# All four heads of a group in every stretch of scores, one PSUM bank for each row quarter

## The chip, the cores and the metric

The kernel runs on one core of one Trainium2 chip. The time is the device time of one execution in microseconds (us); lower is better. An execution is one launch that computes the whole output.

## The reference

The input is x with shape (16, 512, 512): 16 batches of 512 tokens with 512 channels, fp32. The block is attention and a gated feed-forward layer, each between two layer norms:

```python
x = x + layernorm(attention(layernorm(x)))
x = x + layernorm(ffn(layernorm(x)))

# attention, 32 heads of 16 channels
q, k, v = (h @ Wq.T + bq), (h @ Wk.T + bk), (h @ Wv.T + bv)
q, k = rope(rope(q, absolute), temporal), rope(rope(k, absolute), temporal)
scores = q @ k.T / 4                       # causal: -inf above the diagonal
out = softmax(scores) @ v                  # then out @ Wo.T + bo

# ffn, 1408 inner channels; gate, up and down weights are -1, 0 or 1
out = (silu((x @ gate.T) * gate_s) * ((x @ up.T) * up_s)) @ down.T * down_s
```

## The kernel before

**Heads and scores.** A head has 16 channels. Four heads make a group, and there are 8 groups a batch, 128 in all. In SBUF a head stands in 32 of the 128 partitions (a row quarter): q is held as a high and a low part (`q2`), k as two tiles, `kh` and `kl`. So a score matmul has 32 rows, and four of them, one for each row quarter, run in the array side by side. For each head two kinds of scores are computed. `S` (tile `s`, query rows on the partitions) serves only to find each query's maximum: one matmul with `kh`, one with `kl`. `ST` (tile `st`, key rows on the partitions) is what goes into the exponential: `kh`, `kl`, and a third matmul of ones with `mx`, the negated maxima as rows, so that exp needs no other operand. Only blocks on or below the causal diagonal are computed: 512+384+256+128 = 1280 columns for each head and kind.

**Stretches.** A group takes six steps (`STEPS`, `one_step`, L792). In a step, `scores` (L562) handles ST of two heads of group n (`pair`) and S of the other two row quarters' heads of a later group m, n+1 or n+2. A third of the columns is done in a pair of steps (`S_SETS`, `ST_SETS`). `st` has two PSUM banks and one buffer, `s` two buffers of one bank, `av` one bank, and three banks (`ps_d`, tag "d") are shared by all dense products and transposes. After the matmuls, `weights` (L631) takes exp of `st` on ScalarE into `pt` and zeroes the part above the diagonal on GpSimd; `maxima` (L607) adds the mask to `s`, negates and takes the minimum in one custom VectorE operation a block, which is two instructions in the profile (the operation and the read of its accumulator). When all of a group's maxima are there, `turn_maxima` (L617) transposes them on TensorE (`pm`), splits them into two parts (`nmh`, `nml`) and a step later sends them into `mx` by DMA. `values` (L649) multiplies the weights with `v17`, which has a column of ones for the sums, into `av`.

**Dense work.** Between the scores of two steps, and before `values`, stands a share of the other work. `dense`, `gate_ups` and `downs` write it as a list of pieces with costs (an fp32 matmul of 512 columns is 1.0, an fp32r one 0.27, a transpose 0.15), and `run_list` (L696) hands out equal shares of the sum over a batch's 48 steps. The list of batch b holds, in this order: v and q products of batch b+1, o (the attention's output product) of b-1, k of b+1 with the transposes for the feed-forward layer of b-1, gate/up of b-1, down of b-1 with the norm of b+2. A `merge` puts follow-up work on the other engines a given cost later. The tail of a q or k product (`qk_block`, L329) is two bias operations into `ys` on ScalarE, the product with the cosines into `ya` on VectorE and with the sines on GpSimd; its rest adds the two and splits the sum (`yh`, `yl`). The tail of a gate product is tanh on ScalarE and a product on VectorE, that of an up product one VectorE operation into `ht`.

**Order.** Every instruction is kept in program order on its engine (`InOrder`, L39; its line 49 is the line that the profile shows for nearly all instructions). Queue, buffers and order are therefore fixed by the sequence in which the Python code emits them. All loads and stores but three are issued by SyncE (SP).

**Weights.** `load_w` (L227) loads a projection in two halves of 512 KB into four buffers "w"; `load_wf` (L398) loads gate and up weights of 128 inner channels, 512 KB, into three buffers "wf".

**Two arms.** `front` prepares batches 0 and 1 and checks that the three ternary matrices are exact in fp32r; the kernel then runs one of two arms of the program. The profiled one is the `exact` arm, in which gate/up and down are pairs of fp32r matmuls with high and low parts (`xntf`, `xntfl`; `hh`, `hl`).

Of the kernel before, what the change touches and what calls it, by code (L numbers as in the profile page):

```python
# [28 lines left out]
STEPS = 6  # L29
# [5 lines left out]
S_SETS = [[(3, 0, 512)], [(0, 384, 128), (2, 0, 384)], [(1, 0, 256)]]  # L35
ST_SETS = [[(0, 0, 512)], [(3, 0, 128), (1, 128, 384)], [(2, 0, 256)]]
# [17 lines left out]
class Block:  # L54
# [15 lines left out]
    def __init__(self, tc, ctx, a):  # L70
# [15 lines left out]
        self.ps_s = pool("ps_s", bufs=2, space=bass.MemoryType.PSUM)  # L86
        self.ps_t = pool("ps_t", bufs=1, space=bass.MemoryType.PSUM)
# [22 lines left out]
    def constants(self):  # L110
# [13 lines left out]
        for half in range(2):  # L124
            self.load_w(0, "q", half)
        for tb in range(NB):
            self.load_x(1, tb, "x1", 4)
        for half in range(2):
            self.load_w(0, "k", half)
# [5 lines left out]
        for name in ("bo", "dscale"):  # L135
# [6 lines left out]
        self.mask = con.tile([P, T], mybir.dt.bfloat16, tag="mask", name="mask")  # L142
        nc.gpsimd.memset(self.mask, 0.0)
        m = self.mask[:, T - P : T]
        nc.gpsimd.affine_select(
            out=m, in_=m, compare_op=ALU.is_ge, fill=-BIG, base=0, pattern=[[-1, P]], channel_multiplier=1
        )
# [19 lines left out]
        self.odd = con.tile([P, 2 * self.NF], FP, tag="odd", name="odd")  # L167
# [5 lines left out]
    def load_checks(self):  # L173

        a, n = self.a, 2 * NC * P
        ht = self.tile([P, self.NF, T], "ht", bufs=1).rearrange("p f t -> p (f t)")
        xl = self.tile([P, NC, T], "xntfl", bufs=1).rearrange("p c t -> p (c t)")
        places = [ht[:, ts(i, n)] for i in range(self.NF * T // n)] + [xl[:, ts(i, n)] for i in range(NC * T // n)]
        small = [tag for tag, k in (("oc", 4), ("q2", 3), ("kh", 3), ("kl", 3)) for _ in range(k)]
        self.wgu0, self.wd0 = [], []  # L180

        def load(f):
            w = places.pop() if 3 <= f < self.NF - 1 else self.tile([P, n], "wf", bufs=3)
            self.sp.dma_start(out=w, in_=a["wgu"][f].rearrange("p w c j -> p (w c j)"))
            self.wgu0.append(w)

        for f in range(self.NF - 1):
            load(f)
        for f in range(self.NF):
            tag = small.pop()  # L190
            w = self.tile([P, C], tag, bufs=4 if tag == "oc" else 3)
            self.sp.dma_start(out=w, in_=a["wd"][ts(f, P), :])
            self.wd0.append(w)
        self.load_last = lambda: load(self.NF - 1)

    def check_weights(self):

        def check(i, w, r):  # L200
            self.act.copy(r, w)
            self.dve.scalar_tensor_tensor(w, w, 1.0, r, ALU.mult, ALU.not_equal, accum_out=self.odd[:, i : i + 1])

        def gate_up(f):
            if f == 1:
                self.load_last()
            w = self.wgu0[f]
            check(f, w, self.tile(list(w.shape), "pt", bufs=4, dtype=FR))

        def down(f):  # L210
            check(self.NF + f, self.wd0[f], self.wd[:, f, :])
# [15 lines left out]
    def load_w(self, b, name, half):  # L227

        t = self.tile([P, NC, C // 2] if name in "qk" else [P, NC // 2, C], "w", bufs=4)
        self.sp.dma_start(out=t, in_=self.a["w" + name][half])  # L230
        self.wts[b, name, half] = t
# [73 lines left out]
    def v_block(self, b, tb):  # L305
# [6 lines left out]
        return self.product("pv", NC, lambda c: self.xnts["a", b][:, c, ts(tb, P)], lambda c: self.wts[b, "v", c // 2][:, c % 2, :], tail)  # L312

    def fold_bias(self):
# [3 lines left out]
        def tail(p):  # L318
# [6 lines left out]
            lambda c: self.wts[-1, "o", c // 2][:, c % 2, :],  # L325
# [3 lines left out]
    def qk_block(self, b, name, c):  # L329
# [20 lines left out]
        def store():  # L350
# [10 lines left out]
            "p" + name, NC, lambda i: self.wts[b, name, c // 2][:, i, ts(c % 2, P)], lambda i: self.xnts["a", b][:, i, :], tail  # L361
        ), rest, store

    def o_block(self, b, tb):
# [19 lines left out]
        def rest_3():  # L384
# [5 lines left out]
            "po", NC, lambda c: self.ocs[b, c][:, ts(tb, P)], lambda c: self.wts[b, "o", c // 2][:, c % 2, :], tail  # L390
# [7 lines left out]
    def load_wf(self, b, f):  # L398
        if self.exact:
            t = self.tile([P, 2, NC, P], "wf", bufs=3, dtype=FR)  # L400
            self.sp.dma_start(out=t.bitcast(FP), in_=self.wgs[f])
        else:
            t = self.tile([P, 2, NC, P], "wf", bufs=3)
            self.sp.dma_start(out=t, in_=self.a["wgu"][f])
        self.wfs[b, f] = t

    def gate_up(self, b, f):
# [14 lines left out]
        if self.exact:  # L422
            x = lambda i: self.xnts["f", b][i % 2][:, i // 2, :]
            w = lambda k: (lambda i: self.wfs[b, f][:, k, i // 2, :])
# [3 lines left out]
        g = self.product("pg", NC, lambda c: self.wfs[b, f][:, 0, c, :], x, tail_g)  # L428
        u = self.product("pu", NC, lambda c: self.wfs[b, f][:, 1, c, :], x, tail_u)
# [67 lines left out]
    def dense(self, b, between=()):  # L497
# [13 lines left out]
        if nxt:  # L511
            for tb in range(NB):
                L += self.v_block(bn, tb)
            for c in range(NC):
                if c < 2:
                    do(self.load_w, o, "o", c)
                qk("q", c)
                if c % 2:
                    do(self.load_w, bn, "k", c // 2)
        else:  # L520
            for half in range(2):
                do(self.load_w, o, "o", half)
        later = []
        if old:
            do(self.load_xr, o, 0)
            do(self.load_xr, o, 1)
            for tb in range(NB):
                items, *rests = self.o_block(o, tb)
                L += items
                for r, k in zip(rests, (3.5, 6.5, 9.5)):  # L530
                    if r is rests[2] and tb >= 2 and nxt:
                        later.append(r)
                    else:
                        self.merge(L, r, k, ("f", tb))
        L += between
# [26 lines left out]
    def scores(self, n, m, i):  # L562

        third, pair = divmod(i, 2)
        ps = pm = None
        todo = []
        if 0 <= n < self.B * NG:
            ps = self.ps_t.tile([P, 2, T], FP, tag="st", name="st")
            q, ks, mx = self.qs[n], self.ks[n], self.mxs[n]
            for j in range(2):  # L570
                h = 32 * (2 * pair + j)
                r, r2 = slice(h, h + 32), slice(h, h + 2)
                todo.append([])
                for kb, at, w in ST_SETS[third]:
                    out, x = ps[:, j, at : at + w], q[r, T - w : T]
# [3 lines left out]
                        (out, self.one[r2, :], mx[r2, T - w : T], False, True),  # L579
                    ]  # L580
        if 0 <= m < self.B * NG:
            if n < 0 and i % 2:
                both = self.ps_t.tile([P, 2, T], FP, tag="st", name="st")
                pm = [both[:, j, :] for j in range(2)]
            else:
                pm = [self.ps_s.tile([P, T], FP, tag="s", name="s") for _ in range(2)]
            q, ks = self.qs[m], self.ks[m]
            for j in range(2):
                h = 32 * (2 * (1 - pair) + j)
                r = slice(h, h + 32)  # L590
                todo.append([])
                for qb, at, w in S_SETS[third]:
                    out, x = pm[j][:, at : at + w], q[r, ts(qb, P)]
                    todo[-1] += [(out, x, ks[0][r, 0:w], True, False), (out, x, ks[1][r, 0:w], False, True)]

        for k in range(max((len(t) for t in todo), default=0)):
            for t in todo:
                if k < len(t):
                    out, l, r, first, last = t[k]
                    self.pe.matmul(out, l, r, start=first, stop=last)  # L600
        if ps is not None:
            self.weights(n, third, pair, ps)
        if pm is not None:
            for j in range(2):
                self.maxima(m, third, 2 * (1 - pair) + j, pm[j])

    def maxima(self, m, third, j, s):  # L607
        if m not in self.nms:
            self.nms[m] = self.tile([P, 4, NB], "nm", bufs=2)
        for qb, at, w in S_SETS[third]:  # L610
            x = s[:, at : at + w]
            self.dve.tensor_tensor_reduce(
                out=x, in0=x, in1=self.mask[:, T - w : T], scale=-1.0, scalar=BIG, op0=ALU.add, op1=ALU.min,
                accum_out=self.nms[m][:, j, qb : qb + 1],
            )

    def turn_maxima(self, m):  # L617
        p = self.psum("pm")
        self.pe.transpose(p[0:16, 0:P], self.nms.pop(m).rearrange("p j b -> p (j b)"), self.ident)
# [11 lines left out]
    def weights(self, n, third, pair, ps):  # L631
        w = sum(w for _, _, w in ST_SETS[third])
        if third < 2 or pair == 0:
            pt = self.tile([P, 2, T], "pt", bufs=4)
            self.pts[n, third, pair] = pt
        if third == 2:
            if pair:
                pt = self.pts[n, 2, 1] = self.pts[n, 2, 0]
            pt = pt[:, pair, :].rearrange("p (j t) -> p j t", j=2)
        self.act.activation(pt[:, :, :w], ps[:, :, :w], AF.Exp, scale=0.25)  # L640
        if third == 1:
            d = pt[:, :, 0 : 2 * P]
            pat = [[0, 2], [0, 2], [1, P]]
        else:
            d = pt[:, :, 0:P]
            pat = [[0, 2], [1, P]]
        self.pool.affine_select(out=d, in_=d, compare_op=ALU.is_ge, fill=0.0, base=0, pattern=pat, channel_multiplier=-1)

    def values(self, n, third):  # L649
        b, g = divmod(n, NG)  # L650
        if third == 0:
            self.avs[n] = self.ps_av.tile([P, T], FP, tag="av", name="av")
        av = self.avs[n]
        for kb, at, w in ST_SETS[third]:
            for j in range(4):
                h = 4 * g + j
                pt = self.pts[n, third, j // 2]
# [381 lines left out]
```

## Time and profile before

| | before |
|---|---|
| median of 3 runs | 3214.8 us (3213.17 to 3222.2) |
| the profiled execution's own time | 3215.86 us |
| its span in the profile | 3214.0 us |
| granted TensorE clock | 0.984 |
| TensorE busy | 96% |
| VectorE, ScalarE, GpSimd busy | 59%, 48%, 43% |
| DMA, share of 16 engines | 43.1% |
| score matmuls with `s` and `st` | 10212 |
| exp `pt<-st`, 128x1024 and 128x512 | 512 of 1024 ns, 256 of 596 ns |
| maxima `s<-s,mask`, and accumulator reads | 2034 of 510 ns, 2048 of 141 ns |

PE is TensorE's matmuls, PEld its weight loads (they run beside matmuls), DVE VectorE, ACT ScalarE, POOL GpSimd, SP the queue that issues DMAs. A group's name is output<-inputs by the program's tile names. A row's busy time is the union of its instructions' times; the mean of one includes its pipeline latency, so for matmuls that follow each other the distance of their starts says more than their length. Times in a timeline are microseconds from the span's start.

### The profile page before, as it was taken

To read this page: it belongs to the slowest core of one execution; us is meant where nothing else is said; L and a number is where in the kernel's file an instruction comes from. 1 tells how busy PE (TensorE), PEld (TensorE's weight loads), DVE (VectorE), ACT (ScalarE), POOL (GpSimd) and SP (SyncE) were. 2 spreads that over 40 slices of the span, in tenths; PEclk is the share of its full clock that TensorE was granted. 3 is DMA by queue.
4 is the path that set the end of the run, shared out by engine and by line. 5 is a ranking of instruction groups with operands and counts; after the bars stand their busy time and mean duration, and the time that the engine had idled before them with its cause. 6 is when DMAs were issued, how large, how long until landed. Compare 5 with 4: busy or idle time off the path is not lost.

```text
span 3214.0 us, 59287 instructions
## 1 busy us (share of the span) xinstructions
PE 3097.9 (96%) x21258; PEld 1743.3 (54%) x21258; DVE 1888.0 (59%) x5911; ACT 1542.7 (48%) x2243; POOL 1383.9 (43%) x1933
## 2 busy tenths in 40 slices
PE   6889999999999999999999999999999999999988
PEld 2334555646556464655646455464655646455556
DVE  5465656556565665656566565665656566565633
ACT  5354545454554544545454554544455454453432
POOL 4143445443544534345443544534345453443343
PEclk9899999999999999999999999999999999999999
DMA  6454534445353443525345352543535345343422
GB/s 251 166 166 152 189 101 163 139 149 172 108 190 106 160 164 123 195 93 177 127 152 173 127 185 96 168 147 123 195 101 183 122 147 172 123 156 105 131 97 71
DMA packets 227441, 471.41 MB, mean 147 GB/s; under 512 B 40976, under 2 KB 45072, under 8 KB 226704
## 3 DMA queue, kind: packets, MB, share of 16 engines
q1 hardware_dynamic: 226704, 466.47, 43.1%
q8 instruction: 170, 2.79, 0.4%
q10 hardware_dynamic: 432, 1.05, 0.1%
q14 instruction: 135, 1.11, 0.1%
HBM read 345.79 MB, written 125.30 MB: 147 GB/s over the span
## 4 chain that ended last, share of the span: by engine, by line
PE 83%; DVE 2%; DMA 2%; ACT 2%; POOL 1%; issue 1%; SPq 0%; ACTq 0%; DVEq 0%; POOLq 0%
PE st L49 16%; PE pu L49 11%; PE pg L49 10%; PE av L49 9%; PE pd L49 9%; PE po L49 7%; PE pq L49 6%; PE pv L49 5%; PE pk L49 5%; PE s L49 3%; DMA kl<-kd 2%; PE px L49 1%; ACT pt L49 1%; DVE s L49 1%; PE pm L49 1%
## 5 line engine op out<-in xcount | busy, mean ns | idle before, releaser
L49 DVE CUSTOM_DVE_ANT_0 s<-s,mask 128x512 f32<-128x512 f32 (+1 forms) x2034 | 974.9, 510 | 713.8 <-PE s L49 530.8
L49 ACT ACTIVATE pt<-st 128x1024 f32<-128x1024 f32 (+1 forms) x768 | 677.0, 882 | 755.9 <-PE st L49 746.9
L49 POOL TENSOR_SCALAR_AFFINE_SELECT pt<-pt 128x256 f32<-128x256 f32 (+1 forms) x768 | 393.8, 513 | 1202.3 <-ACT pt L49 1200.0
L49 PEld LDWEIGHTS st<-q,kh 32*128 32x128 f32 x2048 | 191.3, 183 | 463.3 <-issue 225.6
L49 PE MATMUL st<-q,kh 32*128 32x512 f32 (+3 forms) x2048 | 411.2, 398 | 22.3 <-ACT pt L49 20.9
L49 PE MATMUL s<-kh,q 32*128 32x512 f32 (+1 forms) x2034 | 411.6, 399 | 17.2 <-DVE nm L49 8.8
L49 PE MATMUL s<-kl,q 32*128 32x512 f32 (+1 forms) x2034 | 340.7, 321 | 11.2 <-DMA kl<-kd 11.2
L49 PE MATMUL av<-pt,v 128*32 128x512 f32 (+3 forms) x4096 | 336.0, 447 | 0.0
L49 PE MATMUL st<-q,kl 32*128 32x512 f32 (+3 forms) x2048 | 333.5, 322 | 0.0
L49 PE MATMUL st<-mx,one 2*128 2x512 f32 (+3 forms) x2048 | 333.0, 321 | 0.0
L49 POOL TENSOR_TENSOR hl<-ht,hh 128x512 fp32r<-128x512 f32 (+1 forms) x192 | 229.6, 1196 | 184.3 <-ACT hh L49 176.7
L49 PE MATMUL pd<-wd,hl 128*128 128x512 f32 x704 | 288.9, 410 | 9.2 <-POOL hl L49 9.2
L49 PE MATMUL pd<-wd,hh 128*128 128x512 f32 x704 | 290.9, 413 | 2.2 <-ACT hh L49 2.2
L49 DVE DVE_READ_ACCUMULATOR2_ANT nm<- 128x1 f32 x2048 | 288.8, 141 | 0.0
L49 PE MATMUL pg<-xntf,wf 128*128 128x512 f32 x704 | 287.4, 408 | 1.5 <-ACT xntf L49 1.5
L49 PE MATMUL pu<-xntfl,wf 128*128 128x512 f32 x704 | 284.3, 404 | 0.0
L49 PE MATMUL pu<-xntf,wf 128*128 128x512 f32 x704 | 283.9, 403 | 0.0
L49 PE MATMUL pg<-xntfl,wf 128*128 128x512 f32 x704 | 281.5, 400 | 0.6 <-DVE xntfl L49 0.6
L49 PE MATMUL po<-w,oc 128*128 128x512 f32 x512 | 244.6, 610 | 3.7 <-DMA w<-in_wo 3.7
L49 PE MATMUL pq<-xnta,w 128*128 128x512 f32 x480 | 237.6, 626 | 6.9 <-ACT xntf L49 6.3
L49 PE MATMUL pk<-xnta,w 128*128 128x512 f32 x480 | 238.3, 615 | 4.3 <-DVE ya L49 3.7
L49 POOL TENSOR_TENSOR yl<-ya,yh 128x512 fp32r<-128x512 f32 x128 | 163.3, 1276 | 169.4 <-ACT yh L49 169.4
(118 smaller groups left out, 5021.8 us busy)
## 6 DMA issues: line engine op xcount, KB each, us to landing
wf<-wgs SPq DMA_DIRECT2D x176, 512.0 KB
q<-qd SPq DMA_DIRECT2D x128, 256.0 KB
kh<-kd SPq DMA_DIRECT2D x128, 256.0 KB
kl<-kd SPq DMA_DIRECT2D x128, 256.0 KB
od<-ot SPq DMA_DIRECT2D x128, 256.0 KB
w<-in_wo SPq DMA_DIRECT2D x34, 512.0 KB
xr<-in_x SPq DMA_DIRECT2D x66, 256.0 KB
w<-in_wq SPq DMA_DIRECT2D x32, 512.0 KB
```

What stands on the lines that cost most here:

```text
L49: return self.tc.keep_in_program_order(f(*args, **kwargs))
```

## The change

The six steps of a group become five. In each, `scores` does S and ST for all four heads: 256 columns of S and 256 of ST in each of the four row quarters, S first. All of it goes into one tile `sc` of four banks with one buffer, one bank for each row quarter; ST has the lower half of each bank, S the upper half. `S_PARTS` and `ST_PARTS` cut the 1280 columns into five parts of 256; step i does ST part i and S part (i+3) mod 5. In ST part 3 and S part 3 the 256 columns are two blocks of 128.

`maxima` is now a `tensor_reduce` with maximum and negation over all four heads (1024 elements of a partition), after an addition of the mask to the diagonal blocks in parts 1, 3 and 4 (512, 1024 and 512 elements); block 0's two halves are joined by a small minimum. It is emitted ahead of the exp of the same step. `weights` is one exp of 1024 elements a step into `pa` (two buffers of two parts each) or, for the last part, `pc` (one buffer of one part), and GpSimd zeroes four blocks at once in four of five steps. `values` follows in two lots, at steps 2 and, for the group before, 0.

To make room in SBUF, weights come in quarters of 256 KB: `load_w` in four pieces into seven buffers, `load_wf` gate and up apart into five, with the places of the loads in the lists moved to suit. The front's checks of the ternary weights use the new buffers. Delays counted in steps are adapted.

```diff
-STEPS = 6
+STEPS = 5
-S_SETS = [[(3, 0, 512)], [(0, 384, 128), (2, 0, 384)], [(1, 0, 256)]]
-ST_SETS = [[(0, 0, 512)], [(3, 0, 128), (1, 128, 384)], [(2, 0, 256)]]
+HALF = T // 2
+ST_PARTS = [[(0, 0, 256, 0)], [(0, 256, 256, 0)], [(1, 128, 256, 0)], [(1, 384, 128, 0), (3, 384, 128, 128)], [(2, 256, 256, 0)]]
+S_PARTS = [[(3, 0, 256, 0)], [(3, 256, 256, 0)], [(2, 0, 256, 0)], [(0, 0, 128, 0), (2, 256, 128, 128)], [(1, 0, 256, 0)]]
+ST_DIAG = [0, None, 0, 128, 0]
...
-        self.ps_s = pool("ps_s", bufs=2, space=bass.MemoryType.PSUM)
-        self.ps_t = pool("ps_t", bufs=1, space=bass.MemoryType.PSUM)
+        self.ps_sc = pool("ps_sc", bufs=1, space=bass.MemoryType.PSUM)
...
+        self.sc = self.ps_sc.tile([P, 4, T], FP, tag="sc", name="sc")
...
     def scores(self, n, m, i):
...
+        part = (i + 3) % STEPS
+        at_s = HALF if n >= 0 or i % 2 else 0
+        for j in range(4):
+            r, r2 = slice(32 * j, 32 * j + 32), slice(32 * j, 32 * j + 2)
+            todo.append([])
+            if 0 <= m < self.B * NG:
+                q, ks = self.qs[m], self.ks[m]
+                for qb, k0, w, at in S_PARTS[part]:
+                    at += at_s
+                    out, x = self.sc[:, j, at : at + w], q[r, ts(qb, P)]
+                    todo[-1] += [(out, x, ks[0][r, k0 : k0 + w], True, False), (out, x, ks[1][r, k0 : k0 + w], False, True)]
+            if st:
+                q, ks, mx = self.qs[n], self.ks[n], self.mxs[n]
+                for kb, q0, w, at in ST_PARTS[i]:
+                    out, x = self.sc[:, j, at : at + w], q[r, q0 : q0 + w]
                     todo[-1] += [
                         (out, ks[0][r, ts(kb, P)], x, True, False),
                         (out, ks[1][r, ts(kb, P)], x, False, False),
-                        (out, self.one[r2, :], mx[r2, T - w : T], False, True),
+                        (out, self.one[r2, :], mx[r2, q0 : q0 + w], False, True),
                     ]
...
+            self.maxima(m, part, self.sc[:, :, at_s : at_s + HALF])
+        if st:
+            self.weights(n, i)
...
+    def maxima(self, m, part, s):
...
+        if part in (1, 3, 4):
+            d = s if part == 3 else s[:, :, P:HALF]
+            mask = self.mask[:, 0 : d.shape[-1]].unsqueeze(1).to_broadcast(list(d.shape))
+            self.dve.tensor_tensor(d, d, mask, ALU.add)
...
+        self.dve.tensor_reduce(out=out, in_=s, axis=AX.X, op=ALU.max, negate=True)
+        if part == 4:
+            self.dve.tensor_tensor(nm[:, 0, :, 2:4], nm[:, 0, :, 2:4], nm[:, 1, :, 0:2], ALU.min)
...
+    def weights(self, n, i):
+        if i % 2 == 0:
+            self.pts[n, i // 2] = self.tile([P, 4, HALF], "pc", bufs=1) if i == 4 else self.tile([P, 4, T], "pa", bufs=2)
+        at = HALF * (i % 2)
+        pt = self.pts[n, i // 2][:, :, at : at + HALF]
+        self.act.activation(pt, self.sc[:, :, 0:HALF], AF.Exp, scale=0.25)
+        at = ST_DIAG[i]
+        if at is not None:
+            d = pt[:, :, at : at + P]
+            self.pool.affine_select(
+                out=d, in_=d, compare_op=ALU.is_ge, fill=0.0, base=0, pattern=[[0, 4], [1, P]], channel_multiplier=-1
+            )
...
-        t = self.tile([P, NC, C // 2] if name in "qk" else [P, NC // 2, C], "w", bufs=4)
-        self.sp.dma_start(out=t, in_=self.a["w" + name][half])
+        t = self.tile([P, NC, P] if name in "qk" else [P, C], tag, bufs=bufs)
+        self.sp.dma_start(out=t, in_=self.a["w" + name][k])
...
-            t = self.tile([P, 2, NC, P], "wf", bufs=3, dtype=FR)
-            self.sp.dma_start(out=t.bitcast(FP), in_=self.wgs[f])
+                t = self.tile([P, NC, P], "wf", bufs=5, dtype=FR)
+                self.sp.dma_start(out=t.bitcast(FP), in_=self.wgs[f, :, k])
...
-        if i == 3 and 0 <= n < self.B * NG:
+        if i == 2 and 0 <= n < self.B * NG:
             self.values(n, 0)
         if i == 0 and 0 <= n - 1 < self.B * NG:
             self.values(n - 1, 1)
-            self.values(n - 1, 2)
...
-        work = self.run_list(self.first_list(), 56)
+        work = self.run_list(self.first_list(), 46)
```

## The prediction

> **What bounds the kernel now.** I read the page's busy times first, then the busy time by stage, then the timeline around single score stretches, because only those show what one stretch costs.
>
> ```profile
> span 3214.0 us, 59287 instructions
> PE 3097.9 (96%) x21258; PEld 1743.3 (54%) x21258; DVE 1888.0 (59%) x5911; ACT 1542.7 (48%) x2243; POOL 1383.9 (43%) x1933
> ```
>
> PE is busy 96% of the span; no other engine passes 59%. The chain of waits has the same landmark, a wait for `kl<-kd`, at 456.19 us and at 2758.09 us, twelve batches apart: 191.8 us a batch, 23.98 us a group. One batch, cut into its dense stages (v, q, o, k, gate/up, down; columns: length, then busy time of PE, PEld, DVE, ACT, POOL):
>
> ```profile
> 1412.00:1432.00 20.00, 18.95 (x130) 8.33 (x129) 6.75 (x27) 7.76 (x12) 4.97 (x7) 1.00 0.33 103
> 1433.00:1455.00 22.00, 22.00 (x146) 9.65 (x145) 11.55 (x35) 12.05 (x18) 9.55 (x11) 1.00 0.45 145
> 1455.00:1476.50 21.50, 21.50 (x135) 9.43 (x136) 15.84 (x52) 9.78 (x15) 11.61 (x19) 1.00 0.52 174
> 1477.00:1501.00 24.00, 23.35 (x158) 10.89 (x157) 18.29 (x56) 16.60 (x25) 16.58 (x22) 1.00 0.50 171
> 1501.00:1566.00 65.00, 65.00 (x499) 43.90 (x497) 39.48 (x114) 27.56 (x39) 15.65 (x23) 1.00 0.56 187
> 1566.00:1601.00 35.00, 34.41 (x257) 23.23 (x255) 21.26 (x76) 19.99 (x32) 26.14 (x37) 1.00 0.22 75
> ```
>
> PE has nothing to gain from waits here; it gains only if its own work shrinks, and it loses whatever new wait is put in front of it. The reader should note DVE in the o and k stages: 74 to 76% busy, with in-order work.
>
> What one score stretch costs (PE timeline; start, length):
>
> ```profile
> 1502.06 0.39 PE L49 MATMUL pg<-xntf,wf 128*128 128x512 f32 x1
> 1502.38 0.39 PE L49 MATMUL st<-q,kh 32*128 32x256 f32 x2
> 1502.39 0.38 PE L49 MATMUL s<-kh,q 32*128 32x256 f32 x2
> 1502.61 0.28 PE L49 MATMUL st<-q,kl 32*128 32x256 f32 x2
> 1502.61 0.28 PE L49 MATMUL s<-kl,q 32*128 32x256 f32 x2
> 1502.72 0.28 PE L49 MATMUL st<-mx,one 2*128 2x256 f32 x2
> 1502.93 0.50 PE L49 MATMUL pg<-xntfl,wf 128*128 128x512 f32 x1
> ```
>
> Two `st` and two `s` heads start together in four row quarters, but `st` has three matmuls and `s` two, so in the last level two quarters are idle. From first score to next dense start: 0.55 us here, 0.89 us with 512 columns (1510.50 to 1511.39), 1.05 us in the 128+384 stretch (1514.13 to 1515.18). Going in costs 0.09 us more: pg to st is 0.32 us, where dense follows dense after 0.23.
>
> **What the Trainium skill says.** "TensorE: Matmul & The Clock Gate", LDWEIGHTS: a weight load takes its columns over 1.2 GHz, whatever the rows, so 107 ns for 128 columns. The trace agrees: narrow levels start 0.11 us apart (1514.29, 1514.40, 1514.51), 128 columns wide or 256. "PSUM — Partial Sum Buffer", PSUM bank collisions: two engines must not touch one bank and partition quadrant at once, even in different columns, even both reading. The trace before can't show it, as `s` and `st` have banks of their own; the change puts them into one. "VectorE: DVE Perf Modes", perf-mode tier table and errata section: `tensor_reduce` runs at 1x, and an fp32 two-input op takes (N+151)/0.96 ns. The trace agrees for PSUM sources (`x<-po,bo`, 512 elements, 684 ns; formula 691).
>
> **The change part by part.**
>
> PE, scores. Columns stay 1280 for each head and kind in a group. All four quarters now have work at every level. A regular stretch has five levels of 256: 0.55 + 2 x 0.11 = 0.77 us. Stretch 0 (part 3, four narrow S levels) has seven: 0.99. Stretch 3 (six narrow ST levels) has eight: 1.10. Group: 3 x 0.77 + 0.99 + 1.10 + 5 x 0.09 = 4.85 us, against 2 x (0.55 + 0.89 + 1.05) + 6 x 0.09 = 5.52. **Gain 0.67 us a group, 5.4 us a batch, 86 us for 128 groups.** Value matmuls (av) and dense products keep their number.
>
> DVE, maxima. Before, 16 custom ops (714, 567, 447, 312 ns) and 16 accumulator reads (141 ns): 10.4 us a group. After: five reduces of 1024 elements, no row before has one, formula 1.22 us; mask adds of 512, 1024 and 512 (0.69, 1.22, 0.69); one minimum of 0.17. Sum 8.9. ACT: five exps of 1.024 us instead of four and two of 0.596, -0.2 us. POOL: four masks of 0.638 instead of four of 0.450 and two of 0.638, -0.5 us. All three lie beside PE, worth nothing by themselves.
>
> The new wait. In the changed instruction order every exp waits for the reduce of its own stretch, and the next stretch's first matmul waits for that exp; before, exp waited for PE only and `s` had other banks. So PE's scores -> DVE mask+reduce (D) -> ACT exp -> PE scores is one serial chain a stretch. Behind the waiting exp on ACT stand the casts and biases of the dense products, and DVE ops wait for those. D by stretch 0 to 4: 2.5, 1.95, 1.22, 1.95, 1.22 (mean 1.77). With about 0.08 us a handover (the first maximum starts at 1511.33, 0.09 us after its last `s` matmul ended) and 0.16 at PE's end, a stretch can follow T+1.34+D after the last. Cover is the dense share: 130 us of a batch's PE time that is neither scores nor av, less turns, over 40 stretches, 3.0 us, plus 1.5 (av of 24, 1509.07 to 1510.50) in stretch 0 and 0.7 to 1.1 in stretch 2. Bare, that is level: short by 0.2 us in stretches 1 and 3, to spare elsewhere. What decides is what DVE and ACT have ahead of it.
>
> q stage. The order is exp, yh cast, two ys biases (ACT), ya product (DVE), next reduce. The trace before shows the link, exp to next maximum 3.48 us after it:
>
> ```profile
> 1443.55 1.02 ACT L49 ACTIVATE pt<-st 128x1024 f32<-128x1024 f32 x1 [1.49 <-PE st L49]
> 1444.73 1.39 ACT L49 ACTIVATE ys<-pq,cols 64x512 f32<-64x512 f32 x2
> 1446.21 0.75 DVE L49 SCALAR_TENSOR_TENSOR ya<-pq,cols,turn 128x512 f32<-128x512 f32 x1 [0.96 <-POOL pt L49]
> 1447.03 0.30 DVE L49 CUSTOM_DVE_ANT_0 s<-s,mask 128x128 f32<-128x128 f32 x1
> ```
>
> Before, it ended there. Now D and the next exp follow: 1.02 + 0.62 (yh) + 1.39 + 0.75 + 0.27 handovers = 4.05, plus D, 5.8 us a stretch with a product end, against PE's 4.4. Four product ends: 4 x 5.8 + 0.6 x 3.9 = 25.6 us for the 4.6 stretches of the stage, PE needs 20.4; less 0.7 of initial slack, **4.5 us lost**. k stage: the same and an `xntfl` subtraction (0.68) on DVE: 4 x 6.5 + 1.3 x 3.9 = 31 against 23.5; less slack **6.5 us**. gate/up, 13.6 stretches: exp, tanh 0.69, DVE product 0.69 and `ht` 0.75 ahead of the reduce; worked stretch by stretch in its order I get stalls of 0.2, 0.7, 1.0, 0.25 a group. The 1.0 is new in kind: the transposed maxima (pm) hold one of three product banks until ACT has copied them behind the exp. 2.15 a group with leftovers of the k stage; I take 1.5, **4 us** for 2.7 groups (0 to 6). o stage: by the same working 1.1 a group, **1 us**. down: `hh` casts behind the exp make `hl` late (its wait was 9.2 us in all), **2 us** (0.5 to 4). v: **0.4 us**. Sum 18.4 us against 5.4: **+13 us a batch**, fourteen full batches +182. The last batch's gate/up and down, +8. Batch 0 has little dense cover and is bound by such chains already (48 stretches from 104 to 275 us, 3.56 us each; after, T+1.34+D and the scores give 20.4 us a group, with tails about the 21 of before): 0, bounds -10 to +10. Profiled run 3215.9 + 190 = 3406, median 3214.8: **3405 us**.
>
> Loads. Weights in quarters: 130 more w and 176 more wf issues of 0.33 to 0.5 us, about 120 us on SP, which issues for 1136 of 3214 us: hidden. The wf ring now blocks SP until the gate product ends, delaying mx, q, k loads queued behind by up to 2.5 us; they have two stretches (9 us) to spare. 0, bounds -4 to +20 (kl waits were 11.2 us on PE). The front's smaller checks: 0, -5 to +5.
>
> **The rivals.** (A) Faster: chunks and tails fall so that the serial chain stays under cover. For it: bare, the chain is within 0.2 us of cover, PE is the bound everywhere, DVE has 1.5 us less. Against: q and k loops use durations and an order that leave no room. With all but 20 to 60 us hidden: 3150 to 3190. It decides if stalls stay below 5.4 us a batch. (B) Only q and k stall: 11 - 5.4 = 5.6 a batch, 3295. (C) The reduce over four banks costs more than 1.22, say 1.5: five longer links a group, up to +1.4 us, 3550. (D) Four matmul pairs in 0.11 us is more than PE issues, so no gain: +86, 3490; against it, 1514.29 and 1514.40 show two full levels 0.11 apart.
>
> **How the numbers follow.** A run tells 0.3% from no change. Main case 0.53 (3340 to 3470), B 0.25 (3240 to 3340), C or D 0.05, A 0.14, within 0.3% of before 0.03. Faster 0.14, same 0.03, slower 0.83. Range 3210 to 3480: it leaves out A's and C's far ends.
>
> **What would show it.** Right: PE waits of 1 us and more at the `sc<-kh` matmuls, ended by the exp (`pa`, `pc`), most in q and k; exp's idle ended by DVE (`nm`); a PE share near 90%; regular stretches of 0.77 us; a batch of about 205 us. Wrong: a batch under 191 us with PE still at 96%; exp starting within 1.5 us of the last score; stalls at weights or `mx` instead.

## The result, and the profile after

| | before | after |
|---|---|---|
| median | 3217.2 us (3213.17 to 3222.2, 4 runs) | 3500.2 us (3485.18 to 3505.13, 4 runs) |
| span of the profiled execution | 3214.0 us | 3502.8 us |
| a full batch (mean of 13) | 191.8 us | 208.2 us |
| TensorE idle, same 13 batches, each | 2.3 us | 18.3 us |
| TensorE busy, same 13 batches, each | 189.5 us | 189.9 us |
| granted TensorE clock, whole execution | 0.984 | 0.958 |

The ratio is 1.0871, 95% interval 1.0834 to 1.0908: slower by 283 us. The forecast was slower by 190, and its range ended at 3480.

The busy times on the page of after:

```profile
span 3502.8 us, 66653 instructions
PE 3102.7 (89%) x26378; PEld 1838.4 (52%) x26378; DVE 1992.3 (57%) x2973; ACT 1506.1 (43%) x2118; POOL 1323.0 (38%) x1678
```

Every engine's share has gone down: nobody has become the bound, everybody waits more. PE's own 3102.7 us are no fewer than the 3097.9 before, although its scores are packed more densely; why is told below. The busy time by stage (v, q, o, k, gate/up, down; length, then PE, PEld, DVE, ACT, POOL; behind them the granted TensorE clock, the DMA share and GB/s):

```profile
1338.30:1359.80 21.50, 20.62 (x161) 9.63 (x158) 9.37 (x11) 7.45 (x11) 3.32 (x5) 1.00 0.38 124
1359.80:1384.70 24.90, 21.70 (x186) 10.20 (x184) 11.86 (x15) 12.06 (x18) 10.20 (x11) 1.00 0.52 159
1384.70:1412.70 28.00, 24.10 (x193) 11.31 (x189) 18.87 (x35) 11.09 (x15) 12.91 (x20) 0.94 0.34 107
1412.70:1440.30 27.60, 23.59 (x182) 11.44 (x178) 17.26 (x27) 14.61 (x21) 14.16 (x17) 0.94 0.45 148
1440.30:1508.40 68.10, 64.67 (x598) 45.98 (x597) 41.06 (x53) 26.94 (x37) 14.69 (x17) 0.97 0.54 175
1508.40:1547.30 38.90, 35.11 (x346) 24.60 (x344) 24.41 (x44) 20.93 (x32) 26.93 (x37) 1.00 0.21 70
```

Before, PE was busy for all but 0.7 us of any stage from q on. Now each of these stages holds 3 to 4 us of PE idle, and the o stage lost as much as any. The clock in o and k is 0.94, where it was 1.00. What a stretch of scores costs PE, on its timeline in the down stage:

```profile
1524.69 0.39 PE L53 MATMUL sc<-kh,q 32*128 32x256 f32 x4
1524.91 0.29 PE L53 MATMUL sc<-kl,q 32*128 32x256 f32 x4
1525.03 0.28 PE L53 MATMUL sc<-q,kh 32*128 32x256 f32 x4
1525.15 0.28 PE L53 MATMUL sc<-q,kl 32*128 32x256 f32 x4
1525.27 0.28 PE L53 MATMUL sc<-mx,one 2*128 2x256 f32 x4
1525.48 0.49 PE L53 MATMUL pd<-wd,hl 128*128 128x512 f32 x1
```

Four heads a level, five levels, the second 0.22 us behind the first and the others 0.12 us apart, 0.79 us from first score to next dense start: the packing does what was forecast (0.77). The loss is in the waits (engine, what it waited for, us in all, times, longest; first two lines of before, then two of after):

```profile
ACT pt L49 <- PE st L49: 746.9, 485, 6.5
...
PEld st L49 <- ACT pt L49: 79.3, 105, 2.3
```

```profile
ACT pa L53 <- DVE nm L53: 1275.1, 485, 5.2
...
PEld sc L53 <- ACT pa L53: 357.5, 301, 4.1
```

Before, exp (`pt`) waited for PE, and weight loads of `st` waited only 79.3 us in all for exp. Now 485 of the 512 exps into `pa` wait for the maxima (`nm`), and 301 times a weight load of the next stretch waits for such an exp.

### The profile page after: what moved, and what is told of

Its sections match the earlier page's. It is cut to its first block, busy times and chain, and to the rows that moved or that the text cites. A ratio compares the mean times of both kernels' runs of the same rounds, so it can differ in the third digit from the quotient of the medians.

```text
span 3502.8 us, 66653 instructions
## 1 busy us (share of the span) xinstructions
PE 3102.7 (89%) x26378; PEld 1838.4 (52%) x26378; DVE 1992.3 (57%) x2973; ACT 1506.1 (43%) x2118; POOL 1323.0 (38%) x1678
## 5 line engine op out<-in xcount | busy, mean ns | idle before, releaser
L53 ACT ACTIVATE pa<-sc 128x1024 f32<-128x1024 f32 x512 | 524.3, 1024 | 1315.4 <-DVE nm L53 1275.1
L53 DVE TENSOR_REDUCE nm<-sc 128x4 f32<-128x1024 f32 (+1 forms) x640 | 782.1, 1222 | 198.8 <-PE sc L53 185.5
L53 POOL TENSOR_SCALAR_AFFINE_SELECT pa<-pa 128x512 f32<-128x512 f32 x384 | 243.9, 635 | 1372.7 <-ACT pa L53 1314.8
L53 DVE TENSOR_TENSOR sc<-sc,mask 128x512 f32<-128x512 f32 (+1 forms) x384 | 335.8, 875 | 426.5 <-PE sc L53 421.1
L53 PE MATMUL sc<-kh,q 32*128 32x256 f32 (+1 forms) x3072 | 278.0, 361 | 234.1 <-ACT pa L53 174.2
L53 PEld LDWEIGHTS sc<-kh,q 32*128 32x128 f32 x3072 | 151.7, 187 | 627.7 <-ACT pa L53 356.1
L53 PE MATMUL av<-pa,v 128*32 128x512 f32 (+2 forms) x3072 | 283.2, 473 | 0.0
L53 PE MATMUL pv<-w,xnta 128*128 128x512 f32 x460 | 226.2, 630 | 3.7 <-DVE ya L53 3.7
L53 PE MATMUL sc<-mx,one 2*128 2x256 f32 (+1 forms) x3072 | 223.4, 279 | 2.6 <-DMA mx<-nml 2.6
L53 PE MATMUL sc<-q,kh 32*128 32x256 f32 (+1 forms) x3072 | 223.3, 280 | 1.0 <-ACT pa L53 1.0
```

Source lines behind the costliest of these rows:

```text
L53: return self.tc.keep_in_program_order(f(*args, **kwargs))
```

## The experiments

In each, "the chain" is the time from a stretch's first score matmul to the end of its last exp or maximum, the mean over 500 stretches of the trace. The time of "after" is the 3500.2 us above.

**1. Exp ahead of the maxima.** In `scores`:

```diff
-        if 0 <= m < self.B * NG:
-            self.maxima(m, part, self.sc[:, :, at_s : at_s + HALF])
         if st:
             self.weights(n, i)
+        if 0 <= m < self.B * NG:
+            self.maxima(m, part, self.sc[:, :, at_s : at_s + HALF])
```

> The changed kernel with the exp of a stretch emitted ahead of its maxima, nothing else. Theory (serial chain through VectorE, with ScalarE's casts for the dense work queued behind an exp that waits for the reduce): the sum of the chain is the same, but exp starts right after the scores and the casts behind it with it; VectorE now waits for exp instead. About 3290 us, with waits at sc<-kh ended by VectorE (nm) instead of ScalarE. Rival 'the chain's length alone decides': 3470 to 3500, no change. Rival 'weights in quarters and SP's queue decide': 3500, no change.

Measured: 3419.5 us, 1.0639 (1.0599 to 1.0679) of before. The chain is as long as in after (4.43 and 4.44 us), and 81 us come back. So the order on the queues is worth 81 us, not 210: the larger part stays with the length. In the waits VectorE now stands behind exp, and PE behind VectorE:

```profile
DVE sc L53 <- ACT pa L53: 751.2, 364, 5.1
...
PE sc L53 <- DVE nm L53: 188.2, 207, 3.2
```

**2. No mask additions.**

```diff
-        if part in (1, 3, 4):
+        if False:
```

> The changed kernel without the three mask additions of a group (the maximum is then taken over the unmasked scores too). It shortens VectorE's link by 0.70 + 1.23 + 0.70 = 2.6 us a group and nothing else. Theory (serial chain): 3370 to 3400 us, the waits at sc<-kh (233 us) about halved, most of what is left in the stretches without a mask. Rival 'weights in quarters and SP's queue decide': 3490 to 3500.

Measured: 3314.8 us, 1.0313 (1.0283 to 1.0343). The waits of PE at `sc<-kh` fall from 234 to 124 us, as expected, but the time by 185 us, more than the 100 to 130 expected: 1.45 us a group for 2.6 us of length, or 0.55 us for each microsecond of work taken out. The chain is 3.82 us.

**3. No maxima.** `maxima` only sets `nm` to 0, once a group; exp waits for TensorE alone.

```diff
-        if part in (1, 3, 4):
-            ...
-        self.dve.tensor_reduce(out=out, in_=s, axis=AX.X, op=ALU.max, negate=True)
-        ...
+        self.dve.memset(self.nms[m], 0.0)
```

> The changed kernel with the maxima left out (nm is set to 0 by a small memset a stretch; the S matmuls stay), so exp waits for TensorE alone, as before the change. Theory: nothing of the loss is left and TensorE's gain of 4.8 us a batch is: 3130 to 3150 us, TensorE near 96% busy. Rival 'narrow matmuls of all four quarters cost more than they seem': 3220 and above. Rival 'weights in quarters and SP's queue decide': near 3500, with the waits moved to wf, w or kh.

Measured: 3100.9 us, 0.9648 (0.9595 to 0.9701). Its busy times:

```profile
PE 2984.5 (96%) x26378; PEld 1801.9 (58%) x26378; DVE 913.0 (29%) x1949; ACT 1522.5 (49%) x2118; POOL 1334.8 (43%) x1678
```

The packed matmuls, the banks and the weight loads are all still those of after; with VectorE out of the chain (2.42 us now) the whole loss is gone, 400 us, and PE is back at 96%. PE's busy time is 118 us less than in after, for the same 26378 matmuls, at a granted clock of 0.985 instead of 0.958. It ends even below the 3130 expected: batch 0, from its first `mx` scores to the next batch's v products, takes 132 us instead of 188.

**4. The kernel before with the weight loads of after.** Scores, six steps and banks as before; quarters, seven `w` and five `wf` buffers, and the places in the lists as after.

```diff
-        t = self.tile([P, NC, C // 2] if name in "qk" else [P, NC // 2, C], "w", bufs=4)
+        t = self.tile([P, NC, P] if name in "qk" else [P, C], tag, bufs=bufs)
...
-            t = self.tile([P, 2, NC, P], "wf", bufs=3, dtype=FR)
+                t = self.tile([P, NC, P], "wf", bufs=5, dtype=FR)
```

> The kernel before (its scores, six steps, its banks) with the changed kernel's weight loads: quarters, seven buffers w, five wf, the places in the lists. Theory: hidden beside TensorE, 3207 to 3227 us. Rival 'weights in quarters and SP's queue decide': a good part of the 283 us, 3350 or more.

Measured: 3232.3 us, 1.0055 (1.0032 to 1.0078): 17 us, a little over what was expected, and no good part of 283.

**5. Exp and maxima crossed.** The four banks become two tiles of two heads each, and the two engines take them in opposite order.

```diff
-        self.sc = self.ps_sc.tile([P, 4, T], FP, tag="sc", name="sc")
+        self.sc = [self.ps_sc.tile([P, 2, T], FP, tag=f"sc{k}", name=f"sc{k}") for k in range(2)]
...
+        has_m = 0 <= m < self.B * NG
+        for a, b in ((0, 2), (2, 0)):
+            if st:
+                self.weights(n, i, a)
+            if has_m:
+                self.maxima(m, part, self.sc[b // 2][:, :, at_s : at_s + HALF], b)
...
```

> The changed kernel with the four banks as two tiles of two (two heads each) and exp and maxima crossed: ScalarE takes exp of heads 0 and 1 while VectorE takes the maxima of heads 2 and 3, then they change over. The work is the same, cut into twice as many instructions of half the size (about +0.8 us a group on each of the two engines), but exp and maxima of a stretch lie beside each other instead of one behind the other: about 1.2 us less from scores to scores in each of the five stretches, 6 us a group. Theory (serial chain, of which the last experiment without masks gave back 1.45 us a group for 2.6 us of length): most of the loss against the kernel without maxima (400 us) goes, 3180 to 3240 us. Rival 'VectorE's and ScalarE's queues, not the chain, set the pace': the added instructions make it no faster, 3480 or more.

Measured: 3280.1 us, 1.0186 (1.0156 to 1.0215), 220 us under after although VectorE and ScalarE are busier (2129 and 1606 us instead of 1992 and 1506). That is short of the 3180 to 3240 expected. The expected 6 us a group was too much: the chain went from 4.44 to 3.74 us, 3.5 us a group, since half an exp takes 0.60 us and not 0.51, half a maximum 0.69 and not 0.61. A stretch with a mask on the timeline (PE's first scores, then the lines of exp and maxima):

```profile
1489.76 0.39 PE L53 MATMUL sc<-kh,q 32*128 32x256 f32 x4
...
1490.66 0.60 ACT L53 ACTIVATE pa<-sc 128x512 f32<-128x512 f32 x1
1490.80 0.43 DVE L53 TENSOR_TENSOR sc<-sc,mask 128x256 f32<-128x256 f32 x1 [1.42 <-PE sc L53]
1491.26 0.69 DVE L53 TENSOR_REDUCE nm<-sc 128x2 f32<-128x512 f32 x1
...
1491.94 0.42 DVE L53 TENSOR_TENSOR sc<-sc,mask 128x256 f32<-128x256 f32 x1
1492.05 0.60 ACT L53 ACTIVATE pa<-sc 128x512 f32<-128x512 f32 x1 [0.80 <-DVE nm L53]
1492.40 0.69 DVE L53 TENSOR_REDUCE nm<-sc 128x2 f32<-128x512 f32 x1
...
1493.01 0.15 DVE L53 TENSOR_TENSOR nm<-nm 128x4 f32<-128x4 f32 x1
```

The first exp lies beside the first mask addition, the second beside the second mask addition and the start of the second maximum: 3.40 us from scores to the end.

**6. The control: the same instructions in line.** As experiment 5, but the four banks stay one tile, so each half waits for the half before it. Against experiment 5:

```diff
-        self.sc = [self.ps_sc.tile([P, 2, T], FP, tag=f"sc{k}", name=f"sc{k}") for k in range(2)]
+        self.sc = self.ps_sc.tile([P, 4, T], FP, tag="sc", name="sc")
...
-                self.maxima(m, part, self.sc[b // 2][:, :, at_s : at_s + HALF], b)
+                self.maxima(m, part, self.sc[:, b : b + 2, at_s : at_s + HALF], b)
```

> The same instructions in the same order as the crossed kernel (with its masks), but the four banks stay one tile, so that every half waits for the one before it: exp of heads 0 and 1, maxima of 2 and 3, exp of 2 and 3, maxima of 0 and 1, one behind the other. If the crossed kernel (3280 us) gained by exp and maxima lying beside each other: the chain is about 0.5 us a stretch longer than with exp first (3420 us), 2.6 us a group, at the slope of the run without masks some 185 us, 3550 to 3650. If it gained by the new order or the smaller pieces alone: 3270 to 3330.

Measured: 3745.1 us, 1.1657 (1.1600 to 1.1714). The same kind of stretch on its timeline:

```profile
1491.81 0.39 PE L53 MATMUL sc<-kh,q 32*128 32x256 f32 x4
...
1492.72 0.60 ACT L53 ACTIVATE pa<-sc 128x512 f32<-128x512 f32 x1 [0.19 <-PE sc L53]
1493.35 0.43 DVE L53 TENSOR_TENSOR sc<-sc,mask 128x256 f32<-128x256 f32 x1 [0.58 <-ACT pa L53]
...
1493.82 0.69 DVE L53 TENSOR_REDUCE nm<-sc 128x2 f32<-128x512 f32 x1
...
1494.54 0.60 ACT L53 ACTIVATE pa<-sc 128x512 f32<-128x512 f32 x1 [1.23 <-DVE nm L53]
...
1496.25 0.15 DVE L53 TENSOR_TENSOR nm<-nm 128x4 f32<-128x4 f32 x1
```

Same durations, one behind the other: 4.59 us instead of 3.40. The mean chain is 5.05 us against 3.74, and 465 us lie between two kernels that differ in nothing else: 3.6 us a group for 6.5 us of length. It is overlap, not order or size of pieces, that experiment 5 gained by. The expectation was too low: the chain is 0.62 us a stretch longer than in experiment 1, not 0.5, and the time rose by 326 us, where the slope of experiment 2 gives 218. A longer chain costs more for each microsecond. Part of the 326 us is a slower PE: the same 26378 matmuls keep it busy for 86 us longer than in experiment 1 (3145.3 and 3059.1 us), at a granted clock of 0.947 instead of 0.971.

**7. Crossed, without mask additions.** Experiment 5 with experiment 2's edit.

> As the crossed kernel, without the mask additions (the maximum is taken over the unmasked scores too). If the chain from scores to scores still ends at sc<-kh: 1.3 us a group less length, 40 to 100 us under the crossed kernel. If the crossed chain is already covered by the dense work: within 20 us of it.

Measured: 3169.7 us, 0.9843 (0.9814 to 0.9871): 110 us under experiment 5, a little more than expected; the chain is 3.01 us. This is faster than both kernels, than before by 1.6%. It takes the maximum over the unmasked scores of a diagonal block too; that is at least the visible maximum, and a softmax is the same for any shift as long as its exps don't vanish, so the version suits inputs whose hidden scores don't lie far above the visible ones. A variant in which GpSimd zeroes all four heads in one instruction again (in `weights`, when the second half is done):

```diff
-        if at is not None:
-            d = pt[:, :, at : at + P]
+        if at is not None and j == 2:
+            d = self.pts[n, i // 2][:, :, HALF * (i % 2) + at : HALF * (i % 2) + at + P]
```

> The crossed kernel without mask additions, with GpSimd zeroing the four heads of a stretch in one instruction again instead of two: four instructions fewer a group on GpSimd, whose hl waits behind them (waits at pd<-hl are 23 us). 3155 to 3170 us if that is what makes hl late; over 3175 if the weights of heads 0 and 1, now zeroed later, are missed by the value matmuls.

Measured: 3168.1 us, 0.9851 (0.9823 to 0.9880), the same within the interval, and the waits at `pd<-hl` stay at 23 us: those instructions aren't what makes `hl` late.

**8. The transposed maxima earlier or later.** In `one_step`, `turn_maxima` ahead of the third stretch's scores (early), or behind that stretch's dense share (late):

```diff
-        self.scores(n, n + 2 if i >= 2 else n + 1, i)
         if i == 2 and 0 <= n + 1 < self.B * NG:
             self.turn_maxima(n + 1)
+        self.scores(n, n + 2 if i >= 2 else n + 1, i)
```

> The changed kernel with the transposed maxima (pm) emitted ahead of the third stretch's scores, nothing else. The prediction had their held bank cost 1.0 us a group of gate/up work, which is 1.5 us a batch as counted, and PE waits of 24.7 us stand at pm itself. Theory: 3460 to 3475 us. Rival 'pm holds nothing up': 3490 to 3510.

> The changed kernel with the transposed maxima (pm) emitted behind the third stretch's share of dense work instead of ahead of it, the opposite of the early pm, which cost 41 us and had 66 us of waits at pm itself. If what pm costs is its own wait for VectorE's last maximum, which the stretch between now covers: 3460 to 3490 us, waits at pm under 10 us. If it is the bank that pm holds behind an exp: no gain, 3490 to 3510.

> As the crossed kernel, with the transposed maxima (pm) emitted ahead of the third stretch's scores instead of behind them, so that their product bank is free before ScalarE's next exp. If a bank held by pm behind an exp still costs time there: 15 to 40 us under the crossed kernel; if it is covered by now: within 10 us of it; if the earlier transpose waits for the maxima instead: slower by up to 60 us (0.5 us a group).

> The crossed kernel without mask additions (3170 us) with the late pm of the run before. Its waits at pm are 16.5 us in all: 3150 to 3165 us if they go, 3170 to 3185 if the bank held by pm then stops a dense product instead.

All four were slower than the kernels that they change, against what was expected but for the last case named for the crossed kernel. On after: early 3540.9 us (1.0995, 1.0963 to 1.1027), late 3553.6 (1.1050, 1.1018 to 1.1082). On the crossed kernel, early: 3326.9 (1.0331, 1.0295 to 1.0367), 47 us more. Without masks, late: 3230.3 (1.0044, 1.0024 to 1.0063), 61 us more. On after, gate/up did become shorter both ways, 68.0 to 66.6 us a batch, about the 1.5 that the prediction put on the held bank there; but down went from 38.9 to 43.0 (early) and 43.2 (late), k from 27.5 to 28.4 and 30.2, and waits at `pm` from 25 to 66 and 54 us. Also, right behind score matmuls `pm` costs PE about 0.7 us a batch, elsewhere 1.7 to 2.0. In the early version the waits of PE are no longer in all than in after; PE is busy for 43 us more (3145.8 us, granted clock 0.948), as much as the whole loss. Why down and k lose wasn't settled.

## Why the prediction was right in kind and wrong in size

By the kernels' chains, in order of length:

| kernel | chain, us | time, us | PE busy, us | granted clock |
|---|---|---|---|---|
| no maxima (3) | 2.42 | 3101 | 2984.5 | 0.985 |
| crossed, no masks (7) | 3.01 | 3170 | 3008.6 | 0.983 |
| crossed (5) | 3.74 | 3280 | 3031.6 | 0.974 |
| no masks (2) | 3.82 | 3315 | 3025.6 | 0.975 |
| exp first (1) | 4.43 | 3420 | 3059.1 | 0.971 |
| after | 4.44 | 3500 | 3102.7 | 0.958 |
| halves in line (6) | 5.05 | 3745 | 3145.3 | 0.947 |

The last two columns are of the profiled execution; all seven kernels run the same 26378 matmuls.

The time follows the chain, and at equal length (1 and after) the order on the queues makes 81 us. That is the predicted mechanism: a serial chain through VectorE, with casts queued behind the exp that waits. The last two columns show a cost that the prediction doesn't have: from kernel to kernel, where PE waits more, its granted clock is lower in the main and the same matmuls take longer. Between no maxima and after that is 118 of the 397 us between the spans, between exp first and after 44 of 91. No run changed the clock alone, so how much of it the waits cause is read from the traces (last section), not tested.

Rival A (hidden) is refuted: PE's idle time rose by 16 us a batch, not by less than 5.4. B (only q and k stall) is refuted too: all stages from q to down lose. C (a dearer reduce) did not come: the reduce takes 1222 ns, and the formula that "VectorE: DVE Perf Modes" (the errata section) in the Trainium skill gives for an fp32 two-input addition, carried over to 1024 elements of a reduce, makes 1224. D (no matmul gain) is refuted: from start to start, less idle time, score matmuls take 35.9 us of PE a batch instead of 40.7. Loads: 17 us on the kernel before, inside the stated bounds of -4 to +20, where 0 was taken; what they cost within after, where SP's queue moves differently, wasn't isolated.

**PE's gain.** Forecast 5.4 us a batch, measured at the scores 4.8. Stretches of five levels take 0.79 us (forecast 0.77), of seven 1.01 (0.99), of eight 1.06 (1.10). But it did not arrive in PE's busy time. The 13 full batches before and after (columns as in the busy times by stage):

```profile
259.60:2752.70 2493.10, 2463.42 (x17266) 1397.03 (x17264) 1509.96 (x4756) 1237.70 (x1806) 1116.59 (x1557) 1.00 0.44 147
```

```profile
298.30:3005.20 2706.90, 2468.42 (x21428) 1472.88 (x21424) 1595.90 (x2366) 1208.62 (x1702) 1067.45 (x1351) 0.97 0.42 136
```

PE is busy as long as before, at a granted clock of 0.97 instead of 1.00. The clock record of the trace has 136 of these 2707 us at half clock, before 9 of 2493. As half of such time is lost to a busy PE, that is an estimated 5 us a batch, about the gain.

**The chain's bare length.** T+1.34+D with a mean T of 0.88 and D of 1.77, less the last handover to PE, is 3.91 us. The tenth percentile of each of the five kinds of stretch averages 3.90. So the durations were right. What was missed is that the chain is seldom bare: its mean is 4.44, because VectorE and ScalarE have other work in front.

**The stalls by stage.** Measured loss is the stage's change in length, plus its share (by length) of the 4.8 us that PE gained:

| us a batch | v | q | o | k | gate/up | down | sum |
|---|---|---|---|---|---|---|---|
| before | 23.1 | 22.3 | 22.2 | 24.2 | 64.8 | 35.3 | |
| after | 22.1 | 25.0 | 26.7 | 27.5 | 68.0 | 38.9 | |
| loss, measured | -0.4 | 3.3 | 5.1 | 3.9 | 4.8 | 4.5 | 21.2 |
| loss, forecast | 0.4 | 4.5 | 1 | 6.5 | 4 | 2 | 18.4 |

The sum is nearly right, in part by luck: some 5 us of it are the lower clock; PE's idle time alone rose by 16.0. Nor are the parts right. q and k, worked out link by link, were too dear by 1.2 and 2.6; **o** and **down**, dismissed in a sentence, too cheap by 4.1 and 2.5. In the batch shown above, the clock of 0.94 in o is an estimated 1.7 us of its loss (0.06 x 28.0). The o stage on the timeline of after (all engines, lines of one chain):

```profile
1406.35 0.39 PE L53 MATMUL sc<-kh,q 32*128 32x256 f32 x4
...
1407.53 0.70 DVE L53 TENSOR_TENSOR sc<-sc,mask 128x512 f32<-128x512 f32 x1 [0.17 <-PE sc L53]
...
1408.26 1.23 DVE L53 TENSOR_REDUCE nm<-sc 128x4 f32<-128x1024 f32 x1
...
1409.58 1.02 ACT L53 ACTIVATE pa<-sc 128x1024 f32<-128x1024 f32 x1 [4.55 <-DVE nm L53]
...
1410.50 0.81 ACT L53 ACTIVATE xn<-x,ln_sh,ln_rstd 128x512 f32<-128x512 f32 x1
...
1411.36 0.66 PE L53 MATMUL px<-ident,xn 128*128 128x128 f32 x4 [1.97 <-ACT xn L53]
```

ScalarE is idle for 4.55 us in front of the exp. The norm's `xn` stands behind it on the queue, and the transposes `px` wait 1.97 us for `xn`. The prediction had named "the casts and biases of the dense products" behind the exp and left out the norms. PE idles 4.5 us a batch at `px` in after, 0 before, and 0.4 with exp first, which gives the cause: the waiting exp, not the norm.

**The sum.** The two spans differ by 289 us. Full batches: 13 x 16.4 = 214, forecast 13 x 13 = 169. The tail: 36, forecast 13 + 8 = 21. Front and batch 0: 39, forecast **0**. In the full batches the idle time rose by less than the 18.4 forecast; the step that failed there is PE's gain of 5.4, which the prediction took off whole, while PE's busy time rose by 0.4. Batch 0 is the step that failed most for its size. The prediction read 3.56 us a stretch over 48 stretches as "about the 21 of before" a group; from its first `mx` scores to the next v products batch 0 took 151 us before, 18.8 a group, and 188 us after, 23.5. That it is "bound by such chains already" was taken as a reason for no loss, when a longer chain is paid where little covers it: 16.5 a group without maxima, 18.4 crossed, 21.6 with exp first. Batch 0 before and after:

```profile
109.00:259.60 150.60, 127.05 (x975) 54.70 (x969) 83.20 (x297) 68.11 (x95) 51.55 (x75) 0.85 0.50 167
```

```profile
110.40:298.30 187.90, 132.84 (x1296) 64.07 (x1292) 88.67 (x112) 66.47 (x87) 47.46 (x59) 0.75 0.38 127
```

PE idles 55 us of it instead of 24, and its busy time is 6 us longer, at a clock of 0.75 instead of 0.85.

## What to carry to other kernels

Before two kinds of results share one single-buffered set of banks, follow the buffer's way round: the consumers that may not overlap add up to one chain, and here a microsecond more of its mean length cost from 0.2 us (2.42 to 3.01, 69 us over 640 stretches) to 0.8 us (4.43 to 5.05, 326 us), although bare it was level with PE's other work. A wait can cost twice: once as idle time, and again in a lower clock for the work behind it, so compare PE's busy time and granted clock too, and not only its waits. List every kind of instruction that stands behind a newly waiting one, norms included; and if two engines must both read the tile, split it by banks and let them cross, which gave back 220 of 283 us. A stretch of the program with little other work has no slack: there price the chain at its full length.

## What the runs showed of the hardware

Where PE waited, it also ran slower. A stretch in batch 0 of after, on PE's timeline:

```profile
190.07 0.59 PE L53 MATMUL sc<-kh,q 32*128 32x256 f32 x4 [3.22 <-ACT pa L53]
190.45 0.42 PE L53 MATMUL sc<-kl,q 32*128 32x256 f32 x4
190.67 0.42 PE L53 MATMUL sc<-q,kh 32*128 32x256 f32 x4
...
191.09 0.42 PE L53 MATMUL sc<-mx,one 2*128 2x256 f32 x4
```

After 3.22 us of idle the levels are 0.21 us apart, where they were 0.12 at 1524.91, and the five take 1.02 us from first to last start instead of 0.58. Around this wait the granted clock (behind the last bracket) was:

```profile
185.23:188.65 3.42, 1.62 (x22) 0.65 (x14) 3.27 (x6) 0.57 (x1) 2.71 (x4) 1.00 0.38 129
188.65:192.06 3.41, 1.99 (x22) 1.66 (x23) 1.04 (x3) 1.02 (x1) 0.59 (x1) 0.50 0.35 117
```

It fell to half at 188.65, in the middle of the wait (186.85 to 190.07), and was full again at 195.47. "TensorE: Matmul & The Clock Gate" (Part 1) in the Trainium skill says that the array falls to half its clock after an idle window of about 3.4 us. The half agrees: in all traces here the granted clock is 1.00 or 0.50. The idle window doesn't: in the 3.42 us in front of this fall PE was busy for 1.62, and the measurement decides. In the trace of after, PE was busy for at most 67% of the 3.41 us in front of each of the 59 falls later than 100 us, for at most 42% in half of them; of 871 such windows without a fall, only 3 were busy for less than half. So 1.8 us of waiting out of 3.42 were enough here. Half clock makes 102 us of before, 297 of after, and 96 instead of 45 us of batch 0. That waits bring the clock down is what these traces show together; no run tested it apart from the waits.

Two engines in different banks at the same time do not disturb each other here: with exp and maxima crossed, half a mask addition takes 0.43 us with an exp beside it (1490.80) and 0.43 in line without (1493.35), and the exp 0.60 in both. "PSUM — Partial Sum Buffer" (PSUM bank collisions) forbids accesses at the same time to one bank in the same partitions only; no run had both engines in one bank at once.
